# Halo copies of a four-layer convolution kernel: from three bursts per image to one or two copies per pair of tiles

## The chip, the cores and the metric

The kernel runs on one core of one Trainium2 chip. The metric is the device time of one launch in microseconds, as the median of several runs. The engines are named as in the profile: PE (TensorE), DVE (VectorE), ACT (ScalarE), POOL (GpSimd) and SP (SyncE, which only issues DMAs here).

## The reference

Four residual layers act on x of shape (T=4, B=8, N=512, D=512), float32; for the last three, the first axis counts images, the second channels, and 512 x 512 are rows and columns:

```
x = x + attention(group_norm(x))         # layer 0
x = x + conv13x13_depthwise(group_norm(x))   # layer 1, reflected borders
x = x + conv3x3_int8(group_norm(x))      # layer 2: x scaled by 127 / max|x| over all, rounded; weights likewise; plus bias
x = x + conv3x3(group_norm(x))           # layer 3: zero padding, plus bias
```

`group_norm` has 4 groups of 2 channels and takes mean and variance over a group's channels and all rows and columns of an image. So layer 3 of an image can begin only when layer 2 of that whole image is done.

## The kernel before

Layers 0 and 1 take the first 2590 us and are not touched. Layer 1 leaves its result in DRAM (`x2d`); layers 2 and 3 work on it together, in the function `layers23`.

An image of 512 rows is cut into 85 windows of 8 rows x 8 channels = 64 partitions; neighbouring windows start 6 rows apart. Two windows lie one above the other in the 128 partitions of a tile, two tiles make a pair, and an image has 22 pairs (`N_PAIRS`; the last holds one window). The result of layer 2 stays in SBUF in `x3`, a ring with places for 26 pairs (`RING`), since layer 3 follows 25 pairs behind (`N_PAIRS + LAG`).

The steps for one pair, with their lines:

- `load` (L949): two DMAs of 256 KB, issued by SP, bring the pair into one of six `x` buffers, five pairs ahead.
- `quantise`: POOL reorders the columns into `u` (L963, two copies, four `u` buffers), ACT scales them to `y` (L967), DVE rounds them to bf16 `xq` (L972).
- `layer2`: twelve matmuls (L988), then DVE adds the residual and writes `x3` (L993), and takes statistics (L996).
- `layer3`: POOL fills the two border columns (`edge`, L1059), TensorE does the fp32 matmuls (L1066), ACT adds the constant and writes `o` (L1075, six buffers), SP stores it (L1082, two DMAs of about 192 KB).

A 3 x 3 filter on a window of 8 rows gives 6 rows of results. So after layer 2 only the 6 inner rows of a window are right, and its first and last row (the halo) must come from the windows above and below before layer 3 reads them. The function `halos` does this inside SBUF, by DMAs that POOL issues (L1013 and L1014): the first row of each window is copied from the seventh of the window above, and the last row of the one above from the second of this window. One copy serves all windows of one class (the four places `c` in a pair) in a range of pairs; each moves 8 partitions x 2 KB per window. Where a range crosses the end of the ring, `split` cuts the copies into pieces.

Before, the halos of an image are issued in three ranges of pairs, 0 to 10, 11 to 18 and 19 to 21, each at once when its last pair is through layer 2:

```
chunks = [0, 11, 19, N_PAIRS]
if 0 <= t < T and p + 1 in chunks:
    halos(t, chunks[chunks.index(p + 1) - 1], p + 1)
```

After an image's last pair, `norm3` computes its norm in steps between the pairs: sums on DVE and TensorE, a power on POOL (L195), then DVE folds the norm into layer 3's weights (`band_t`, L1035), and TensorE and DVE make a constant (L1044, L1048).

The framework puts the instructions of each engine in an order of its own that keeps the dependences; each engine then runs its list strictly in that order. `n` counts the turns of the main loop: layer 2 of pair `n`, quantising of pair `n + 1`, layer 3 of pair `n - 25`.

Of the kernel before, what the change touches and what calls it, by code (L numbers as in the profile page):

```python
# [43 lines left out]
T, B, N, D, H = 4, 8, 512, 512, 8  # L44
# [20 lines left out]
W_IN, W_STEP, W_ALL = 8, 6, 85  # L65
N_PAIRS = (W_ALL + 3) // 4
# [6 lines left out]
def place(q):  # L73

    p, c = divmod(q, 4)
    return p, c // 2, (c % 2) ^ (c // 2)
# [816 lines left out]
def layers23(  # L893
    s, tc, x2d, out, ident, ind, mask2, avg_same, group_steps, m2, r2, most, w, early, pool
):
    nc = tc.nc
# [44 lines left out]
    def load(t, p):  # L941
        ahead[t, p] = xt = early["x"].tile([P, 2, D], F32, tag="x", name=f"x2_{t}_{p}")
        src = x2d[t]
        first, second = (dict(windows(k)) for k in (2 * p, 2 * p + 1))
        for a, q in first.items():

            n = 2 if a in second else 1
            step = second[a] - q if n == 2 else 1
            nc.sync.dma_start(  # L949
                xt[a * HALF : (a + 1) * HALF, :n, :],  # L950
                bass.AP(
                    src.tensor, src.offset + q * W_STEP * B * D,
                    [[D, HALF], [step * W_STEP * B * D, n], [1, D]],
                ),
            )

    def quantise(t, p):
        n, n_p = len(tiles(p)), HALF * len(windows(tiles(p)[-1]))
        x = ahead.pop((t, p))[:n_p, :n, :]
        u = early["u"].tile([P, 2, D], F32, tag="u", name="u2")  # L960
        y = early["y"].tile([P, 2, D], F32, tag="y", name="y2")
        for j in range(n):
            nc.gpsimd.tensor_copy(  # L963
                u[:n_p, j, :].rearrange("p (v g) -> p v g", g=PH),
                x[:, j, :].rearrange("p (g v) -> p v g", g=PH),
            )
        nc.scalar.activation(  # L967
            y[:n_p, :n, :], u[:n_p, :n, :], AF.Identity, bias=w["mr"][:n_p, t : t + 1],
            scale=w["r"][:n_p, t : t + 1],
        )  # L970
        xq = w["xq"][(t * N_PAIRS + p) % 3]
        nc.vector.tensor_scalar(  # L972
            xq[:n_p, :n, 2 : D + 2], y[:n_p, :n, :], ROUND, ROUND, op0=ALU.add, op1=ALU.subtract
        )
        ready[t, p] = u, xq

    def layer2(t, p):
        ks = tiles(p)
        n_p = HALF * len(windows(ks[-1]))
        u, xq = ready.pop((t, p))  # L980
        s0 = slot(t, p)
        st3 = w["st3"][t % 2]
        for j, k in enumerate(ks):
            ps = ps_2.tile([P, D], F32, tag="conv2", name="ps_conv2")
            for dx in range(3):
                for a, _ in windows(k):
                    half = slice(a * HALF, (a + 1) * HALF)
                    mm = nc.tensor.matmul(  # L988
                        ps[half, :], lhsT=w["band2"][half, 0, dx, :], rhs=xq[half, j, dx + 1 : dx + 1 + D],
                        start=dx == 0, stop=dx == 2,  # L990
                    )
            own = x3[:n_p, s0 + j, 1 : D + 1]
            nc.vector.scalar_tensor_tensor(  # L993
                own, ps[:n_p, :], w["inv"][:n_p], u[:n_p, j, :], op0=ALU.mult, op1=ALU.add
            )
            nc.vector.bn_stats(st3[:n_p, k, :], own)  # L996
        return mm.ins
# [3 lines left out]
    def halos(t, p0, p1):  # L1001


        for c in range(4):
            first = max(p0, 1) if c == 0 else p0
            n = min(p1, (W_ALL - c + 3) // 4) - first
            _, j, a = place(c)
            before, j_b, a_b = place(c + 3)
            for q0, q1, n_q in split(t, first, n, before - 1):
                here = pairs[a * HALF : (a + 1) * HALF, q0 : q0 + n_q, j, :]  # L1010
                there = pairs[a_b * HALF : (a_b + 1) * HALF, q1 : q1 + n_q, j_b, :]
                end = (W_IN - 1) * B
                nc.gpsimd.dma_start(here[:B], there[W_STEP * B : (W_STEP + 1) * B])  # L1013
                nc.gpsimd.dma_start(there[end : end + B], here[B : 2 * B])  # L1014

    def split(t, p, n, back):

        while n > 0:
            q0, q1 = slot(t, p) // 2, slot(t, p + back) // 2
            now = min(n, RING - q0, RING - q1)  # L1020
            yield q0, q1, now
            n, p = n - now, p + now

    def norm3(t):


        st3 = w["st3"][t % 2].rearrange("p k (h z) -> p (k h) z", z=3)
        nc.vector.tensor_scalar_add(st3[:, :, 1], st3[:, :, 1], w["b2"])
        m, r = yield from group_steps(
            st3.unsqueeze(1), 1, W2_N * 2, mask2, avg_same, ps_1, f"x3_{t}"  # L1030
        )
        zero = wpool.tile([P, 1], F32, tag="zero", name="zero")
        nc.vector.tensor_sub(zero, m, w["b2"])
        band = wpool.tile([P, 2, 3, HALF], F32, tag="band", name="band_t")
        nc.vector.scalar_tensor_tensor(  # L1035
            band, w["band3"], r, w["eye3"], op0=ALU.mult, op1=ALU.add
        )
        scaled = wpool.tile([P, 1], F32, tag="scaled", name="scaled")
        nc.vector.tensor_mul(scaled, zero, r)
        yield  # L1040
        ps = ps_1.tile([P, 1], F32, tag="misc", name="ps_const")
        for a in range(2):
            half = slice(a * HALF, (a + 1) * HALF)
            nc.tensor.matmul(  # L1044
                ps[half, :], lhsT=w["sum3"][half, a, :], rhs=scaled[half, :], start=True, stop=True
            )
        const = wpool.tile([P, 1], F32, tag="const", name="const")
        nc.vector.tensor_sub(const, w["b23"], ps)  # L1048
        norms[t] = zero, band, const
        yield  # L1050

    def layer3(t, p, zero, band, const):


        ks = tiles(p)
        s0 = slot(t, p)
        n_p = HALF * len(windows(ks[-1]))
        edge = x3[:n_p, s0 : s0 + len(ks), 0 : D + 2 : D + 1]
        nc.gpsimd.tensor_copy(edge, zero[:n_p].unsqueeze(2).to_broadcast([n_p, len(ks), 2]))  # L1059
        ps = [ps_3.tile([P, D], F32, tag="conv3", name="ps_conv3") for _ in ks]  # L1060
        for dx in range(3):
            for j, k in enumerate(ks):
                for a, q in windows(k):
                    half = slice(a * HALF, (a + 1) * HALF)
                    b = 1 if q == W_ALL - 1 else a ^ j
                    nc.tensor.matmul(  # L1066
                        ps[j][b * HALF : (b + 1) * HALF, :], lhsT=band[half, b, dx, :],
                        rhs=x3[half, s0 + j, dx : dx + D],
                        start=dx == 0, stop=dx == 2,
                    )  # L1070
        for j, k in enumerate(ks):
            q = 4 * p + 2 * j
            used = slice(HALF if q == W_ALL - 1 else 0, P)
            o = early["o"].tile([P, D], F32, tag="o", name="o3")
            nc.scalar.activation(o[used], ps[j][used], AF.Identity, bias=const[used])  # L1075
            row, n = q * W_STEP + 1, 2 * W_STEP
            at = 2 * B
            if q == 0:
                row, n, at = row - 1, n + 1, at - B
            if q == W_ALL - 1:  # L1080
                n, at = W_STEP + 1, HALF
            nc.sync.dma_start(  # L1082
                out[t, :, row : row + n, :].rearrange("c r w -> r c w"), o[at : at + n * B, :]
            )

    chunks = [0, 11, 19, N_PAIRS]
    n_all = T * N_PAIRS
    norms, norm = {}, iter(())  # L1090
    for n in range(n_all + N_PAIRS + LAG):
        if n < n_all:
            for m in range(6) if n == 0 else [n + 5]:
                if m < n_all:
                    load(*divmod(m, N_PAIRS))
            for m in range(2) if n == 0 else [n + 1]:
                if m < n_all:
                    quantise(*divmod(m, N_PAIRS))
            did = layer2(*divmod(n, N_PAIRS))
        next(norm, None)  # L1100
        t, p = divmod(n - 1, N_PAIRS)
        if 0 <= t < T and p + 1 in chunks:
            halos(t, chunks[chunks.index(p + 1) - 1], p + 1)
        if n >= N_PAIRS + LAG:
            t, p = divmod(n - N_PAIRS - LAG, N_PAIRS)
            with tc.issue_after(did):
                layer3(t, p, *norms[t])
        if n < n_all and n % N_PAIRS == N_PAIRS - 1:
            norm = norm3(n // N_PAIRS)
        next(norm, None)  # L1110
# [36 lines left out]
```

## Time and profile before

| What | Value |
|---|---|
| Time, median of 3 runs | 3078.7 us (3075.29 to 3078.77) |
| Span of the profiled execution | 3080.3 us |
| PE, DVE, POOL, ACT busy over the whole span | 95%, 73%, 34%, 16% |
| Layer 2 alone | about 2600 to 2698 us |
| Layers 2 and 3 together | about 2698 to 3003 us |
| Layer 3 alone | about 3003 to 3077 us |
| Halo copies | 126, of 16 to 176 KB, about 0.59 us of POOL each |

The busy shares are averages over stages with different limits: TensorE is full in layers 0 and 1 and less so afterwards. What the change can move is read in the last 480 us. "x<-x" in the DMA lists is a halo copy when POOL issues it, and a load of `x2d` (or of layer 1's input) when SP does.

### The profile page before, as it was taken

The numbers are of one execution on the slowest core, as the hardware profiler recorded it, in microseconds if no ns is written. First come the engines' busy times: TensorE is split into PE (matmuls) and PEld (weight loads), VectorE is DVE, ScalarE is ACT, GpSimd is POOL, SyncE is SP. The second block draws the span as 40 slices with busy tenths as digits, with TensorE's granted clock in tenths as the row PEclk, the third lists the DMA queues.
The fourth block names the chain that finished last, engine by engine and source line by source line (L and its number), as shares of the span: only waits on it lengthen the run. The fifth ranks groups of instructions, "written<-read, shape, count | busy, mean of one in ns | idle before, by whom it ended". The sixth has DMA issues, their size and how long they took to land. (4 is left out here: it accounts for less than half of the span.)

```text
span 3080.3 us, 38586 instructions
## 1 busy us (share of the span) xinstructions
PE 2917.2 (95%) x13993; PEld 1467.1 (48%) x13993; DVE 2246.8 (73%) x3761; ACT 481.6 (16%) x657; POOL 1056.4 (34%) x1995
## 2 busy tenths in 40 slices
PE   8999999999999999999999999998999997488789
PEld 6555555555555555555555555554333332144344
DVE  5997688688679768868967876886556556977660
ACT  1300010010000001001001000000112112254444
POOL 1242233333234223333323422332111114766661
PEclk9999999999999999999999999998999999899899
DMA  5221212212222221212211111115778776977775
GB/s 180 75 83 63 74 65 66 66 63 74 65 65 68 63 76 63 67 65 63 79 47 56 49 49 56 46 39 115 212 205 217 203 216 184 167 199 186 195 173 153
DMA packets 276212, 327.35 MB, mean 106 GB/s; under 512 B 24112, under 2 KB 171704, under 8 KB 275797
## 3 DMA queue, kind: packets, MB, share of 16 engines
q1 hardware_dynamic: 211930, 235.77, 28.1%
q0 software_dynamic: 24288, 62.35, 7.4%
q10 hardware_dynamic: 39803, 26.77, 2.9%
q8 instruction: 110, 1.80, 0.2%
q14 instruction: 81, 0.66, 0.1%
HBM read 210.60 MB, written 103.17 MB: 102 GB/s over the span
## 5 line engine op out<-in xcount | busy, mean ns | idle before, releaser
L464 PE MATMUL ps_in<-w_v,xn 128*128 128x512 f32 x1024 | 462.1, 600 | 2.4 <-issue 2.1
L464 PE MATMUL ps_in<-w_k,xn 128*128 128x512 f32 x1024 | 450.2, 592 | 1.1 <-DVE v_k L429 0.7
L464 PE MATMUL ps_in<-xn,w_q 128*128 128x512 f32 x1024 | 449.6, 592 | 0.2
L750 PE MATMUL ps_conv<-x,bt 112*64 112x512 f32 x2048 | 445.0, 593 | 0.0
L500 PE MATMUL ps_b<-toep,vtok 128*64 128x512 bf16 x3072 | 372.3, 383 | 0.0
L549 POOL COPY x1s<-x1s 128x2 f32<-128x2 f32 (+1 forms) x1024 | 227.2, 277 | 295.8 <-DVE x1s L538 295.8
L437 POOL TENSOR_TENSOR h_v<-h_v,c_v 128x512 f32<-128x512 f32 x96 | 123.1, 1283 | 578.9 <-DVE h_v L436 544.4
L412 ACT ACTIVATE h_q<-v_q,c_half 128x512 f32<-128x512 f32 x96 | 69.3, 722 | 1543.7 <-DVE v_q L408 1198.6
L527 PE MATMUL ps_out<-wp,so 128*128 128x512 f32 x1024 | 308.9, 444 | 0.0
L464 PEld LDWEIGHTS ps_in<-w_k,xn 128*128 128x128 f32 x1024 | 194.1, 190 | 222.4 <-issue 205.5
L464 PEld LDWEIGHTS ps_in<-xn,w_q 128*128 128x128 f32 x1024 | 191.8, 190 | 220.1 <-issue 213.1
L464 PEld LDWEIGHTS ps_in<-w_v,xn 128*128 128x128 f32 x1024 | 190.4, 191 | 216.8 <-issue 211.0
L750 PEld LDWEIGHTS ps_conv<-x,bt 112*64 112x64 f32 x2048 | 150.0, 135 | 286.4 <-issue 285.9
L1066 PE MATMUL ps_conv<-x,band_t 64*64 64x512 f32 x2040 | 269.6, 604 | 0.5 <-ACT o L1075 0.3
L500 PEld LDWEIGHTS <-vtok 128*64 128x64 bf16 x3072 | 209.4, 111 | 124.5 <-issue 4.5
L527 PEld LDWEIGHTS ps_out<-wp,so 128*128 128x128 f32 x1024 | 192.6, 188 | 94.1 <-issue 58.3
L963 POOL COPY u<-x 128x512 f32<-128x512 f32 (+1 forms) x172 | 198.5, 1189 | 104.0 <-issue 43.0
L988 PE MATMUL ps_conv<-xq,band 64*64 64x512 bf16 x1020 | 141.7, 411 | 87.7 <-DVE xq L972 86.6
L538 DVE SCALAR_TENSOR_TENSOR x1s<-v_p,xr 128x256 f32<-128x256 f32 x256 | 186.7, 769 | 15.1 <-DMA x<-x1s 3.9
L766 POOL DMA_DIRECT2D x<-xo x128 | 71.4, 565 | 340.6 <-ACT xo L757 326.2
L195 POOL TENSOR_TENSOR grstd_x<-grstd_x,neg_half 128x1 f32<-128x1 f32 (+1 forms) x28 | 21.7, 774 | 429.3 <-DVE grstd_x L194 429.3
L437 POOL TENSOR_TENSOR h_k<-h_k,c_k 128x512 f32<-128x512 f32 x96 | 124.5, 1297 | 117.5 <-DVE h_k L436 117.5
(174 smaller groups left out, 3551.1 us busy)
## 6 DMA issues: line engine op xcount, KB each, us to landing
x<-x SPq DMA_DIRECT2D x64, 917.0 KB
x<-x SPq DMA_DIRECT2D x168, 256.0 KB
x<-x1s POOLq DMA_DIRECT2D x128, 262.0 KB, 2.6
x<-in_x SPq DMA_DIRECT2D x128, 256.0 KB
xr<-in_x SPq DMA_DIRECT2D x128, 256.0 KB
out<-o SPq DMA_DIRECT2D x164, 192.0 KB
xs<-in_x SPq DMA_DIRECT2D x112, 256.0 KB
x<-xo ACTq DMA_DIRECT2D x128, 128.0 KB
```

The source lines that it names most:

```text
L412: nc.scalar.activation(h, v, AF.Identity, bias=c_col, scale=0.5)
L437: nc.gpsimd.tensor_add(h, h, c_twice[n])
L464: mm = nc.tensor.matmul(ps, lhsT=lhsT, rhs=rhs, start=k == 0, stop=k == NC - 1)
L500: nc.tensor.matmul(pb[two * DH : (two + 1) * DH, :], lhsT=v[:, c, h * DH : (h + 1) * DH], rhs=toep[z][:, h, u : u + N], start=c == 0 and z ...
L527: nc.tensor.matmul(ps, lhsT=so[:, k, c * P : (c + 1) * P], rhs=wpT[z][:, k, :], start=k == 0 and z == 0, stop=k == NC - 1 and z == 1,)
L538: nc.vector.scalar_tensor_tensor(own, v.rearrange("p (g v) -> p g v", g=PH)[:, two, :], 1.0, by_phase[:, two, :], op0=ALU.is_ge, op1=ALU.add,)
L549: nc.gpsimd.tensor_copy(x1[:, f, u : u + n], x1[:, fm, um - n + 1 : um + 1][:, ::-1])
L750: nc.tensor.matmul(ps[q * M1 : (q + 1) * M1, :], lhsT=bt[:, z, :], rhs=xt[:, w0 : w0 + N_PS1, z : z + NV], start=z == 0, stop=z == SHIFTS - 1,
L766: engine.dma_start(bass.AP(dst.tensor, dst.offset + (q * n_half * W1_OUT * B + b) * D + f * NV, [[B * D, W1_OUT], [W1_OUT * B * D, n_half] ...
L963: nc.gpsimd.tensor_copy(u[:n_p, j, :].rearrange("p (v g) -> p v g", g=PH), x[:, j, :].rearrange("p (g v) -> p v g", g=PH),)
L988: mm = nc.tensor.matmul(ps[half, :], lhsT=w["band2"][half, 0, dx, :], rhs=xq[half, j, dx + 1 : dx + 1 + D], start=dx == 0, stop=dx == 2,)
L1066: nc.tensor.matmul(ps[j][b * HALF : (b + 1) * HALF, :], lhsT=band[half, b, dx, :], rhs=x3[half, s0 + j, dx : dx + D], start=dx == 0, stop= ...
```

## The change

The halos of an image are issued for two halves, pairs 0 to 10 and 11 to 21. `halos` no longer issues its copies but yields them; the main loop keeps the list of a half and issues one or two of it per turn, so many that the list is empty after nine turns (the divisor is 11 - 2), before the next half begins. It is meant to keep POOL and the DMA engines from getting a whole range of copies at once.

```diff
-                nc.gpsimd.dma_start(here[:B], there[W_STEP * B : (W_STEP + 1) * B])
-                nc.gpsimd.dma_start(there[end : end + B], here[B : 2 * B])
+                yield here[:B], there[W_STEP * B : (W_STEP + 1) * B]
+                yield there[end : end + B], here[B : 2 * B]
...
-    chunks = [0, 11, 19, N_PAIRS]
+    n_chunk = N_PAIRS // 2
+    copies, at_once = [], 0
...
-        t, p = divmod(n - 1, N_PAIRS)
-        if 0 <= t < T and p + 1 in chunks:
-            halos(t, chunks[chunks.index(p + 1) - 1], p + 1)
+        if 0 < n <= n_all and n % n_chunk == 0:
+            t, p = divmod(n - n_chunk, N_PAIRS)
+            copies = list(halos(t, p, p + n_chunk))
+            at_once = -(-len(copies) // (n_chunk - 2))
+        for _ in range(min(at_once, len(copies))):
+            nc.gpsimd.dma_start(*copies.pop(0))
```

## The prediction

> **What bounds the kernel now.** I read the page for the order of the stages, then a table by stretches, because the change touches only the last 480 us. Layer 2 starts on TensorE at 2599.93 us. Up to 2698 layer 2 runs alone (25 pairs of tiles), up to 3003 layers 2 and 3 run together (63 pairs), then layer 3 alone (25 pairs). Columns: length, busy time of PE, PEld, DVE, ACT and POOL, TensorE clock, DMA share, GB/s.
>
> ```profile
> 2600.00:2698.00 98.00, 46.62 (x309) 19.37 (x312) 90.69 (x137) 31.78 (x27) 74.50 (x94) 0.82 0.81 151
> 2698.00:3003.00 305.00, 248.23 (x2158) 123.29 (x2156) 214.47 (x331) 143.36 (x179) 197.78 (x257) 0.90 0.79 190
> 3003.00:3077.00 74.00, 72.34 (x633) 36.31 (x629) 7.34 (x20) 36.50 (x54) 8.04 (x31) 1.00 0.58 158
> ```
>
> In undisturbed stretches of the TensorE timeline a pair takes 3.10 us in the first part (2608.44, 2611.54, 2614.65 and on) and 3.87 us in the second (2762.14, 2766.02, 2769.89). So 25 x 3.10 = 78 us became 98, and 63 x 3.87 = 244 us became 305: some 20 and 61 us are lost, while the tail is full. Whatever the change brings must come from these 81 us.
>
> Where are they? First ACT's timeline beside one burst of copies, and TensorE's next line (number in brackets: idle before, and who ended it):
>
> ```profile
> 2728.89 1.32 ACT L1075 ACTIVATE o<-ps_conv,const 128x512 f32<-128x512 f32 x2 [0.19 <-PE ps_conv L1066]
> 2733.75 0.69 ACT L1075 ACTIVATE o<-ps_conv,const 128x512 f32<-128x512 f32 x1 [3.54 <-DMA out<-o]
> 2735.34 0.69 ACT L1075 ACTIVATE o<-ps_conv,const 128x512 f32<-128x512 f32 x1 [0.90 <-DMA out<-o]
> 2743.87 0.69 ACT L1075 ACTIVATE o<-ps_conv,const 128x512 f32<-128x512 f32 x1 [7.84 <-DMA out<-o]
> ```
> ```profile
> 2748.83 2.34 PE L988 MATMUL ps_conv<-xq,band 64*64 64x512 bf16 x10 [8.44 <-DVE xq L972]
> ```
>
> The copies were issued at 2726.7 to 2732.5. After that the output DMAs land late; ACT (L1075) waits for one of the six `o` buffers; the activation `y` (L967) stands behind it on ACT, then `xq`, then TensorE. So the page's "DVE xq" releases a wait that DMA caused. The same picture ends the idle stretches before 2790.62 (7.0 us), 2860.02 (14.65), 2904.27 (4.9) and 2977.54 (15.2); each restart also runs some 2 us at a low clock. Second, the DMA queues in the first 34 us (no copies) and in the burst at 2634 to 2656, both with layer 2 alone (packets, MB, share of 16 engines):
>
> ```profile
> q1 hardware_dynamic: 2502, 4.57, 50.8%
> ```
> ```profile
> q0 software_dynamic: 864, 1.41, 64.5%
> q1 hardware_dynamic: 722, 1.31, 36.9%
> ```
>
> Loads: 4.57 MB in 0.508 x 34 = 17.3 us of all engines, 264 GB/s. Copies: 1.41 MB in 14.2 us, 99 GB/s: dear bytes. Third, GpSimd while the first image's norm is due:
>
> ```profile
> 2673.79 0.56 POOL L1013 DMA_DIRECT2D x<-x  x1 [0.83 <-DVE gsum_x L175]
> 2675.77 0.59 POOL L1014 DMA_DIRECT2D x<-x  x1 [1.42 <-DMA x<-x]
> 2678.27 0.55 POOL L1013 DMA_DIRECT2D x<-x  x1 [1.92 <-DMA x<-x]
> ...
> 2682.96 0.55 POOL L1014 DMA_DIRECT2D x<-x  x1
> 2683.52 2.05 POOL L963 COPY u<-x 128x512 f32<-128x512 f32 x2
> 2685.53 0.57 POOL L195 TENSOR_TENSOR grstd_x<-grstd_x,neg_half 128x1 f32<-128x1 f32 x1
> ```
>
> The variance (L194) is ready at 2676.75, but its power waits on GpSimd until 2685.53: eight copies, some waiting for earlier copies to land, stand before it. DVE then waits for the power at `band_t` (L1035), with the next `xq` behind that, and TensorE idles 11.1 us.
>
> **What the Trainium skill says.** "DMA: Bandwidth & Descriptors", section "Queues, rings and completion order": each DMA engine takes turns between the queues that have work, packet by packet. The trace agrees: q1 keeps moving in the burst, only slower. "SBUF — State Buffer", section "Door 1: The DMA port swizzle": bandwidth depends on how many of 16 ports the partitions reach; by its table a copy to 8 neighbouring partitions reaches two. The 99 against 264 GB/s fit this; no run here isolates it. Same page, "Who interferes with whom": DVE in its fast modes and GpSimd exclude each other. The trace shows `band_t` at 6.54 us beside GpSimd copies, against 0.6 us for the others ((8.4 - 6.5) / 3).
>
> **The change, part by part.**
>
> Number of issues. The ring has 26 places, an image 22 pairs. A half without a wrap needs 4 classes x 2 = 8 copies; a half with a wrap needs 3 + 2 + 2 + 2 = 9 pieces, 18 copies. Halves start at places 0, 11 | 22, 7 | 18, 3 | 14, 25; those at 22, 18 and 25 wrap. Sum 5 x 8 + 3 x 18 = 94 against 126 now (L1013 and L1014 x63 each). 32 fewer x 0.59 us (37.3 / 63) = 19 us of GpSimd, most of it beside TensorE work. Bytes stay the same.
>
> Order. The trace isn't in program order: 21 edge copies (L1059) run in one go at 2692 although the program has one per pair, and ten of the eighteen copies of image 1's first half stand at 2700 to 2716, eight pairs early. An instruction goes when it is ready and its engine is free; program order only breaks ties. Now eight copies with one place in the program precede the next `u` copies, hence the bursts. After the change the `u` copies come first and a copy takes the gaps; at 2700 to 2716 that gave one to three per pair. So I expect a spread, over some four to nine pairs, not an exact one per pair.
>
> First part, burst at n = 11. TensorE reaches pair 17 at 2655.53 instead of 2636.38 + 5 x 3.10 = 2651.9: 3.6 us lost. Spread, GpSimd has 2.6 us of `u` and 0.6 us of a copy per 3.1 us: about 0.1 x 8 = 1 us of loss. Gain some 2 us.
>
> First norm. Copies of pairs 11 to 18 are no longer issued just before it, so those at n = 22 wait for no landing (that was 1.42 + 1.92 + 0.95 + 1.00 us and more), and fewer stand before the power. If none does, the power comes at about 2677, 8 us sooner; if all eight do, at 2673 + 8 x 0.56 + 2.6 = 2680, 5 us sooner. I take 5, since those copies now collide with the start of layer 3.
>
> Second part: layer 3 of the images starts at 2698, 2807, 2920 and 3017.5, so three periods of 109, 113 and 97 us. The floor of TensorE is 21 x 3.87 + 2 = 83. DMA per full period: loads 22 x 0.524 = 11.5 MB and outputs 8.5 MB at 273 GB/s (q1 in the whole part: 50.12 MB in 60.2% of 305 us) make 73 us; copies 2.7 MB at 133 GB/s (q0: 7.38 MB in 18.2%) make 20 us. Together 93 us: when TensorE no longer stops, DMA is the bound, not TensorE. Today it is busy only 79%, because after each stop loads and outputs run dry (the DMA share is 0.13 at 2795 to 2800, and 0.23 at 2925 to 2930). Spread copies avoid most stops; at some 92% use a full period takes about 101 to 102 us. Gains: 8 and 11. The third period has few loads left (14 of 22 pairs: 7.3 MB), and the copies of image 3's second half, which now begin at 2962 just after another burst and belong to its 15 us stop, move mostly behind layer 2, where DMA is at 0.58: DMA need (7.3 + 8.5) / 0.273 + 2.2 / 0.133 = 74 us, so TensorE bounds it at some 80 us; with the norm and restarts 87. Gain 10.
>
> Added waits: a copy waits on GpSimd for the last pair's DVE work, with `u` copies queued behind it; this exists now (0.4 to 2.6 us). The last copy of a second half goes out at n = 29 or 30, its first reader is n = 35 or 36: five pairs, 19 us, against landings of at most 18.2 us now. Hidden, narrowly.
>
> Sum: 2 + 5 + 8 + 11 + 10 = 36 us; 3078.7 - 36 = 3043 us.
>
> **The rivals.** (a) TensorE becomes the only bound: 45 of the 61 us go and 14 of the 20: 3020 us. For it: copies at 2700 to 2716 caused no stop, and spread copies could move faster than 133 GB/s. Against it: the 93 us of DMA work. (b) The bursts form anew, since all copies of a half become ready at once: the second half now has 1.35 MB together instead of 1.0 and 0.35, and only the shorter norm remains: 3073 us, no measurable change. (c) Slower: copies between the `u` copies, 2.6 + 0.2 + 2 x 0.59 = 4.0 us of GpSimd per pair where a half wraps, against 3.87; more than eight in flight, which makes GpSimd wait for landings (it does in bursts now, up to 2.3 us a time) with `u` behind; and last copies landing after their readers are due. Five us in each of three periods gives 3094 us.
>
> **How the numbers follow.** Forecast 0.52, (a) 0.22, (b) 0.10, (c) 0.16. Faster by over 0.2% (6 us): the first two and a part of (b), 0.77; same 0.07; slower 0.16. The range runs from just under (a), 3016, to the milder half of (c), 3085.
>
> **What would show it.** Right: 94 halo copies in place of 126; ACT's wait at L1075 for the output DMA well under its 69.8 us; TensorE's wait at L988 for `xq` well under 86.6 us; the DMA share between 2698 and the end of layer 2 near 0.9; the first power before 2681; the tail still some 2.8 us per pair. Wrong: waits of layer 3's matmuls (L1066) for copies, GpSimd at its limit with ACT waiting for `u` (L963) more than now, or stops of 8 to 15 us in the old places.

## The result, and the profile after

| | before | after |
|---|---|---|
| Median (range) | 3078.67 us (3075.29 to 3078.77) | 3090.01 us (3085.03 to 3090.89) |
| Ratio of after to before, 95% interval | | 1.0036 [1.0019, 1.0054] |
| From layer 2's first matmul to the end, in the profile | 480.4 us | 487.9 us |

The change made the kernel slower by 0.36%, 11 us; 3043 us, 36 us less, had been forecast. The profile of after is of the fastest of its runs, and its layers 0 and 1 happened to end 4.6 us earlier (layer 2 starts at 2595.3 us, against 2599.9). So positions are compared from layer 2's start on. That time is cut into stages at layer 3's first matmul (L1066) of each image on TensorE; the last stage ends with TensorE's last matmul, 5.0 us before the end of the profile:

| Stage, us | before | after | difference | forecast difference |
|---|---|---|---|---|
| Layer 2 alone, up to layer 3 of image 0 | 98.1 | 108.8 | +10.7 | -7 |
| Layer 3 of image 0 to that of image 1 | 109.0 | 98.3 | -10.7 | -8 |
| Image 1 to image 2 | 113.1 | 101.8 | -11.3 | -11 |
| Image 2 to image 3 | 97.2 | 114.6 | +17.4 | -10 |
| Image 3 to the end of TensorE | 58.0 | 59.4 | +1.4 | 0 |

The differences of this one profile add up to 7.5 us; between the medians it is 11.3. The two middle stages did what was forecast. The first and the fourth lost 28 us together, where 17 us of gain were forecast, and these are the two stages to explain.

The table by stretches of after, with the columns of the one before (length; busy PE, PEld, DVE, ACT, POOL; clock, DMA share, GB/s):

```profile
2600.00:2698.00 98.00, 46.64 (x277) 17.64 (x275) 86.04 (x131) 27.59 (x23) 61.87 (x60) 0.74 0.72 133
2698.00:3003.00 305.00, 262.17 (x2170) 127.77 (x2172) 224.87 (x333) 144.92 (x182) 192.84 (x256) 0.92 0.86 197
3003.00:3077.00 74.00, 73.29 (x627) 35.75 (x624) 7.41 (x20) 32.42 (x51) 10.51 (x35) 0.97 0.59 148
```

In the first row the DMA share fell from 0.81 to 0.72, POOL's busy time from 74.5 to 61.9 us and the clock from 0.82 to 0.74: no engine is busier than before (TensorE has 46.6 us in both), and yet the stage takes longer. That points to a chain of steps that wait for each other, and not to a resource at its limit. In the second row the share rose, from 0.79 to 0.86, and the third is as full as it was. The same table for the middle, with the end of layer 2 left out, of before and then of after:

```profile
2700.00:2960.00 260.00, 218.43 (x1898) 109.35 (x1894) 189.53 (x294) 125.64 (x156) 175.40 (x229) 0.91 0.82 201
```
```profile
2700.00:2960.00 260.00, 233.24 (x1976) 116.10 (x1978) 204.29 (x302) 129.05 (x162) 181.50 (x242) 0.94 0.95 214
```

There the DMA engines went from 0.82 to 0.95 busy: the stops of TensorE behind the bursts are gone, but for one, which is shown below. The table of waits from 2595 us on (total, times, longest), of before and then of after:

```profile
PE ps_conv L988 <- DVE xq L972: 86.6, 26, 15.2
ACT o L1075 <- DMA out<-o: 69.8, 22, 13.6
ACT o L1075 <- PE ps_conv L1066: 34.7, 32, 2.0
```
```profile
PE ps_conv L988 <- DVE xq L972: 70.8, 31, 5.2
ACT o L1075 <- PE ps_conv L1066: 70.1, 25, 7.7
ACT o L1075 <- DMA out<-o: 53.4, 24, 9.6
```

TensorE's longest wait for `xq` fell from 15.2 to 5.2 us, but there are more waits. ACT waits less for the output DMA, and twice as long for layer 3's matmuls. So most of the long stops turned into many short ones.

**The short stops of image 0.** TensorE's timeline of after:

```profile
2628.69 1.50 PE L988 MATMUL ps_conv<-xq,band 64*64 64x512 bf16 x12 [1.61 <-DVE xq L972]
...
2643.92 2.77 PE L988 MATMUL ps_conv<-xq,band 64*64 64x512 bf16 x12 [3.95 <-DVE xq L972]
2649.43 2.77 PE L988 MATMUL ps_conv<-xq,band 64*64 64x512 bf16 x12 [2.75 <-DVE xq L972]
2654.95 2.10 PE L988 MATMUL ps_conv<-xq,band 64*64 64x512 bf16 x12 [2.75 <-DVE xq L972]
```

A pair takes 5.5 us (2643.92 to 2649.43 to 2654.95) in place of 3.1. Why is `xq` late? The DVE timeline of after, around the third of these pairs:

```profile
2651.03 0.75 DVE L993 SCALAR_TENSOR_TENSOR x<-ps_conv,inv,u 128x512 f32<-128x512 f32 x1 [1.66 <-PE ps_conv L988]
2651.82 0.69 DVE L996 BATCH_NORM_STATS2 st<-x 128x6 f32<-128x512 f32 x1
2652.43 0.73 DVE L993 SCALAR_TENSOR_TENSOR x<-ps_conv,inv,u 128x512 f32<-128x512 f32 x1
2653.20 0.69 DVE L996 BATCH_NORM_STATS2 st<-x 128x6 f32<-128x512 f32 x1
2653.81 1.08 DVE L972 TENSOR_SCALAR xq<-y 128x1024 bf16<-128x1024 f32 x1
```

and its input in the ACT timeline:

```profile
2643.96 1.24 ACT L967 ACTIVATE y<-u,mr_own,r_own 128x1024 f32<-128x1024 f32 x1 [4.61 <-DVE xq L972]
2649.47 1.24 ACT L967 ACTIVATE y<-u,mr_own,r_own 128x1024 f32<-128x1024 f32 x1 [4.27 <-DVE xq L972]
```

There are two `y` buffers, and each `y` here waits for the rounding that frees one; so the `y` of 2643.96 is read two roundings later, at 2653.81. It was done at 2645.20, 8.6 us before, and DVE stood idle for 1.66 us ahead of 2651.03. The rounding did not lack its operand: it stands in DVE's list behind four instructions, the first of which waits for TensorE. TensorE in turn waits for the rounding. So TensorE and DVE take turns: rounding, matmuls, additions and statistics, next rounding. Before, the list had the rounding of the next pair first. The DVE timeline of before:

```profile
2632.56 0.67 DVE L972 TENSOR_SCALAR xq<-y 128x1024 bf16<-128x1024 f32 x1
2633.15 1.40 DVE L993 SCALAR_TENSOR_TENSOR x<-ps_conv,inv,u 128x512 f32<-128x512 f32 x2
2634.47 1.27 DVE L996 BATCH_NORM_STATS2 st<-x 128x6 f32<-128x512 f32 x2
2635.66 0.67 DVE L972 TENSOR_SCALAR xq<-y 128x1024 bf16<-128x1024 f32 x1
```

**The short stops at the end of layer 2.** ACT's timeline of after:

```profile
2988.12 1.26 ACT L1075 ACTIVATE o<-ps_conv,const 128x512 f32<-128x512 f32 x2 [6.64 <-issue]
2989.28 1.24 ACT L967 ACTIVATE y<-u,mr_own,r_own 128x1024 f32<-128x1024 f32 x1
2998.22 1.26 ACT L1075 ACTIVATE o<-ps_conv,const 128x512 f32<-128x512 f32 x2 [7.71 <-PE ps_conv L1066]
```

and TensorE's in the same place:

```profile
2991.29 2.34 PE L988 MATMUL ps_conv<-xq,band 64*64 64x512 bf16 x10 [3.27 <-DVE xq L972]
2993.86 4.31 PE L1066 MATMUL ps_conv<-x,band_t 64*64 64x512 f32 x22
3001.39 2.34 PE L988 MATMUL ps_conv<-xq,band 64*64 64x512 bf16 x10 [3.23 <-DVE xq L972]
```

Here the same thing happens on ACT: the outputs (L1075) stand ahead of the next pair's `y`, and they wait for layer 3's matmuls, which on TensorE stand behind layer 2's. The chain is output, `y`, `xq`, layer 2, layer 3, output: 10.1 us a pair (2991.29 to 3001.39) in place of 3.87. POOL issued its last `u` at 2977.16 us, so no input was missing.

**One stop of the old kind.** Just before, pair 81 of layer 2 follows pair 80 only after 15.1 us (2947.21 to 2962.35). ACT waits there for an output DMA, with the DMA engines 0.94 busy (2942 to 2960 us), and layer 3's matmuls start again only when that output is done:

```profile
2953.04 0.69 ACT L1075 ACTIVATE o<-ps_conv,const 128x512 f32<-128x512 f32 x1 [9.56 <-DMA out<-o]
```
```profile
2953.83 2.06 PE L1066 MATMUL ps_conv<-x,band_t 64*64 64x512 f32 x4 [5.13 <-issue]
```

This stop is also there in e2 below, where the order is mended (14.8 us between the same pairs, 2930.39 to 2945.14), and it is gone in e8, which has no copies (3.9 us). So mending the order does not remove it.

**The lists themselves.** The order of each engine's list is fixed when the kernel is compiled. Two counts show what moved: for every pair of layer 2, how many later roundings stand on DVE ahead of its addition (L993), and for every turn of layer 3, how many later `y` stand on ACT ahead of its output (L1075). Call this count the lookahead. The instructions of both traces run in exactly this order. One digit per pair, 22 to an image; the ACT rows begin with turn 25, and the last digit of a row is always 0, since no pair follows:

```
DVE, roundings of later pairs ahead of L993 of pair n, n = 0, 1, ...
before   1111111111111021111110 1011222222221022223210 1001222222210222223210 1001222222221022223210
after    1111111111111000000021 1001111132222222222122 2101111132222222221122 2101111132221100000010

ACT, y of later pairs ahead of L1075 of turn n, n = 25, 26, ...
before   3444444321044443210112 4444333210444443210112 4444444321044443210
after    2222443433343332443210 2222444344333322443210 2222444322111000010
```

A zero means that the lookahead is gone for that pair. Before has single or double ones. After has a run of seven on DVE at pairs 13 to 19, where TensorE takes 5.5 us a pair on the mean, and six at pairs 80 to 85, with four on ACT at turns 82 to 85; the pairs behind these four, 83 to 86, take 6.8, 8.9, 9.0 and 10.1 us. The diff touches neither engine: only POOL's copies changed, and the order of the others moved with them.

### The profile page after: what moved, and what is told of

Same layout as the page of the kernel before. It is cut to its first block, busy times and chain, and to the rows that moved or that the text cites. A ratio compares the mean times of both kernels' runs of the same rounds, so it can differ in the third digit from the quotient of the medians.

```text
span 3083.2 us, 38484 instructions
## 1 busy us (share of the span) xinstructions
PE 2934.6 (95%) x13993; PEld 1470.5 (48%) x13993; DVE 2256.5 (73%) x3761; ACT 478.0 (16%) x657; POOL 1041.3 (34%) x1963
## 5 line engine op out<-in xcount | busy, mean ns | idle before, releaser
L1066 PE MATMUL ps_conv<-x,band_t 64*64 64x512 f32 x2040 | 274.5, 613 | 12.4 <-ACT o L1075 6.8
L963 POOL COPY u<-x 128x512 f32<-128x512 f32 (+1 forms) x172 | 201.7, 1203 | 114.3 <-issue 62.7
L988 PE MATMUL ps_conv<-xq,band 64*64 64x512 bf16 x1020 | 154.2, 432 | 76.2 <-DVE xq L972 70.8
L538 DVE SCALAR_TENSOR_TENSOR x1s<-v_p,xr 128x256 f32<-128x256 f32 x256 | 186.4, 768 | 14.8 <-DMA x<-x1s 3.5
L1066 PEld LDWEIGHTS ps_conv<-x,band_t 64*64 64x64 f32 x2040 | 118.5, 137 | 116.7 <-issue 92.9
```

Of the source, the lines that this page charges most:

```text
L538: nc.vector.scalar_tensor_tensor(own, v.rearrange("p (g v) -> p g v", g=PH)[:, two, :], 1.0, by_phase[:, two, :], op0=ALU.is_ge, op1=ALU.add,)
L963: nc.gpsimd.tensor_copy(u[:n_p, j, :].rearrange("p (v g) -> p v g", g=PH), x[:, j, :].rearrange("p (g v) -> p v g", g=PH),)
L988: mm = nc.tensor.matmul(ps[half, :], lhsT=w["band2"][half, 0, dx, :], rhs=xq[half, j, dx + 1 : dx + 1 + D], start=dx == 0, stop=dx == 2,)
L1066: nc.tensor.matmul(ps[j][b * HALF : (b + 1) * HALF, :], lhsT=band[half, b, dx, :], rhs=x3[half, s0 + j, dx : dx + D], start=dx == 0, stop= ...
```

## The experiments

Two theories. In theory A the two losses come from the order of DVE's and ACT's lists, and the copies, once spread, do what the prediction said. In the rival, theory B, the order is only a side effect: the copies between POOL's `u` instructions and in the DMA queues hold up `u`, `y` or `xq`, so that spread copies cost more than bursts. If A holds, putting the rounding back in front, with every copy left where it is, must mend the losses. If B holds, it mends nothing.

Each kernel is compared with the kernel before on the same chip (3077.0 to 3077.9 us), and the ratios are against that. The experiments ran on three chips, so a difference of a few us between two of them is not clear. The table of stages stands after the last of them.

### The rounding ahead of the addition (e1_xq_first)

An edge of order alone, on top of after: DVE's addition of pair n is issued after the rounding of pair n + 1. No instruction is added.

```diff
-        nc.vector.tensor_scalar(
+        rounded = nc.vector.tensor_scalar(
...
-            nc.vector.scalar_tensor_tensor(
-                own, ps[:n_p, :], w["inv"][:n_p], u[:n_p, j, :], op0=ALU.mult, op1=ALU.add
-            )
+            with tc.issue_after(before):
+                nc.vector.scalar_tensor_tensor(
+                    own, ps[:n_p, :], w["inv"][:n_p], u[:n_p, j, :], op0=ALU.mult, op1=ALU.add
+                )
...
-            did = layer2(*divmod(n, N_PAIRS))
+            did = layer2(*divmod(n, N_PAIRS), rounded)
```

> The changed kernel, with one ordering edge more per pair: on DVE, the instruction that writes pair n into the ring (L993) comes after the rounding of pair n+1 (L972). Copies, their places on GpSimd and all work stay. In the order of the changed kernel the rounding of the next pair stands behind the statistics of the pair before for pairs 13 to 19 of image 0 and for 80 to 85. Theory A (the order is the loss): pairs 13 to 19 go back from 5.4 to about 3.2 us, 7 x 2.2 = 15 us; pairs 80 to 85 stay slow, since ACT's order has the same fault there. About 3075 us. Rival B (the copies delay loads and u copies on GpSimd and the DMA engines, whatever the order): no change, 3090 us.

Measured: 3074.62 us, ratio 0.9984 [0.9977, 0.9992]. Layer 2 alone takes 92.8 us (after: 108.8). TensorE's timeline in the place where it took 5.5 us a pair (lines below L972 move down by one or two):

```profile
2647.20 1.50 PE L989 MATMUL ps_conv<-xq,band 64*64 64x512 bf16 x12 [1.64 <-DVE xq L972]
2650.32 1.50 PE L989 MATMUL ps_conv<-xq,band 64*64 64x512 bf16 x12 [1.62 <-DVE xq L972]
```

The pair is back at 3.12 us and the twelve matmuls at 1.50 us, while POOL's trace has the same copies and `u` in the same order as after's up to there. So the loss in image 0 is the order of DVE. The end of layer 2, where ACT's zeros are left, is still slow: 110.4 us between images 2 and 3 (after: 114.6), with pairs 9.0 us apart in the same timeline:

```profile
2978.36 1.28 PE L989 MATMUL ps_conv<-xq,band 64*64 64x512 bf16 x10 [3.26 <-DVE xq L972]
...
2987.34 2.34 PE L989 MATMUL ps_conv<-xq,band 64*64 64x512 bf16 x10 [3.22 <-DVE xq L972]
```

### And the scaling ahead of the outputs (e2_xq_y_first)

As e1, and layer 3 of a turn, its outputs on ACT with it, is issued after the `y` of the next pair:

```diff
-        nc.scalar.activation(
+        scaled = nc.scalar.activation(
...
-            with tc.issue_after(did):
+            with tc.issue_after(did), tc.issue_after(scaled):
```

> As the run before, and also on ACT: the outputs of a turn (L1075) come after the scaling of pair n+1 (L967). Theory A: the six pairs at 8 to 10 us near the end of layer 2 go to about 4.5 us, a further 20 to 25 us: about 3050 us, and the gain of the spread copies in images 1 and 2 stays (periods of 98 and 102 us between the starts of layer 3). Rival B: 3085 to 3090 us.

Measured: 3052.8 us, ratio 0.9913 [0.9898, 0.9928]. The period between images 2 and 3 falls from 110.4 to 91.8 us, and the one before it from 104.5 to 99.2. TensorE's timeline at the end of layer 2:

```profile
2952.91 1.25 PE L989 MATMUL ps_conv<-xq,band 64*64 64x512 bf16 x10
...
2956.79 1.25 PE L989 MATMUL ps_conv<-xq,band 64*64 64x512 bf16 x10
```

3.88 us a pair, with no wait. Two edges of order, no instruction more or less, turn the change from 0.36% slower into 0.87% faster. Theory B could not give this: POOL's order of copies and `u` is the same in the traces of e1 and e2, and DVE's order of roundings and additions too. What differs is ACT's list, where the zeros are gone.

### Spread only in the middle (e3_spread_middle)

Another way to take the runs of zeros away, without an edge: the first half of image 0 and both halves of image 3 go out at once, as bursts, and only those between are spread.

```diff
-            at_once = -(-len(copies) // (n_chunk - 2))
+            at_once = -(-len(copies) // (n_chunk - 2)) if n_chunk < n < 7 * n_chunk else len(copies)
```

> The changed kernel without ordering edges, but the first half of image 0 and everything from pair 77 on are issued at once; the five halves between are spread as in the change. Its order has no run of pairs with the rounding behind the statistics. Theory A: image 0 as long as before or a little shorter, the gain in images 1 and 2 kept, the last period near that of the kernel before: 3055 to 3062 us. Rival B (spread copies cost in themselves): no better than 3080 us.

Measured: 3063.05 us, ratio 0.9948 [0.9933, 0.9962]. In its compiled lists no two zeros follow each other on either engine. Layer 2 alone takes 91.5 us and the period between images 2 and 3 100.2. It came out 1 us above the forecast. That agrees with A: where the run of zeros is gone, the loss of image 0 is gone, and most of that of the last period (after: 114.6). In its place one stop of 17.4 us, before 2955.30, stands behind the burst of image 3. The run says nothing of B by itself, since the copies moved as well.

### Two halves, but as bursts (e4_halves_at_once)

The ranges of the change without its spreading:

```diff
-            at_once = -(-len(copies) // (n_chunk - 2))
+            at_once = len(copies)
```

> Two halves per image as in the change, but each issued at once when its last pair is through: 94 copies, no spread. Theory A, with its second part that bursts are what stops TensorE in images 1 and 2: the order is that of bursts, so no slow run of pairs, but the stops of 8 to 15 us stay: 3065 to 3080 us, and slower than the run with the middle spread. Rival C (the fewer copies are the gain, not the spread): as fast as the run with the middle spread or faster.

Measured: 3073.1 us, ratio 0.9982 [0.9975, 0.9989]. Layer 2 alone takes 89.5 us (before: 98.1): two ranges for three bring that without any spreading. With them the first norm's power comes 82.3 us after layer 2's start, against 85.6 in before and 96.9 in after. The first two image periods stay at 112.7 and 111.0 us, and the long stops are there as in before. TensorE's timeline of e4:

```profile
2741.87 2.34 PE L988 MATMUL ps_conv<-xq,band 64*64 64x512 bf16 x10 [8.81 <-DVE xq L972]
...
2850.41 2.34 PE L988 MATMUL ps_conv<-xq,band 64*64 64x512 bf16 x10 [12.70 <-DVE xq L972]
```

So the two parts of the change do different things: the ranges mend image 0, and the spreading mends the periods from image 0 to 2 (98.3 and 101.8 in after, 102.1 and 102.9 in e3).

### The edges without the change (e5_before_ordered)

The kernel before with both edges of e2.

> The kernel before with both ordering edges (next pair's rounding ahead of L993, next pair's scaling ahead of L1075) and its three bursts. Theory A: the order of the bursts had few such faults, so the gain is small, and the long waits of ACT for output DMAs after each burst stay: 3060 to 3072 us. Rival D (the edges alone are the gain of the second run, the spread adds nothing): 3053 us or less.

Measured: 3084.27 us, ratio 1.0023 [1.0017, 1.003]: a little slower, where a gain was expected. TensorE still stops (7.9, 9.6, 8.2, 10.0 and 12.1 us at 2744, 2786, 2856, 2902 and 2980 us) and ACT waits 69.7 us for the output DMA, as in before (69.8). So the stops behind the bursts are there without any run of zeros, and the edges bring nothing against them. Why the kernel loses 7 us was not settled. The edges paid only with the spread copies.

### Three ranges, spread (e6_thirds_spread)

The ranges of before, with the copies spread over some nine turns. Its compiled DVE list has the longest runs of zeros of all: pairs 13 to 25, 44 to 47, 66 to 69 and 80 to 87.

```diff
-    n_chunk = N_PAIRS // 2
+    chunks = [0, 11, 19, N_PAIRS]
...
-        if 0 < n <= n_all and n % n_chunk == 0:
-            t, p = divmod(n - n_chunk, N_PAIRS)
-            copies = list(halos(t, p, p + n_chunk))
-            at_once = -(-len(copies) // (n_chunk - 2))
+        t, p = divmod(n - 1, N_PAIRS)
+        if 0 <= t < T and p + 1 in chunks:
+            copies += halos(t, chunks[chunks.index(p + 1) - 1], p + 1)
+            at_once = -(-len(copies) // 9)
```

> No ordering edges; the three ranges of the kernel before, its 126 copies spread one or two per pair. In its order the rounding of the next pair stands behind the statistics for 13 pairs of image 0 (13 to 25) and for eight at the end (80 to 87), and for four in a row at the start of images 2 and 3. Theory A, counting 2.3 us for each of the 13 and the same last period as in the changed kernel: some 13 us more than it in image 0, 4 to 8 us more in images 1 and 2 together: about 3105 us. Rival B (cost per copy on GpSimd): 32 more issues x 0.59 us, at most 10 of it seen: 3090 to 3100 us.

Measured: 3113.7 us, ratio 1.0115 [1.01, 1.013], the slowest of all. Layer 2 alone takes 120.8 us, and TensorE's timeline has the 5.5 us step from 2644 to 2661 and again later (2697.47 to 2702.99):

```profile
2655.39 2.77 PE L988 MATMUL ps_conv<-xq,band 64*64 64x512 bf16 x12 [2.75 <-DVE xq L972]
2660.91 2.77 PE L988 MATMUL ps_conv<-xq,band 64*64 64x512 bf16 x12 [2.75 <-DVE xq L972]
```

More zeros, more loss, at the pairs where the list has them. That holds in the first two image periods too, which are 14 and 10 us longer than after's: behind the zeros at 44 to 47, the additions (L993) of pairs 45 to 48 follow each other after 6.7, 8.7, 9.1 and 9.1 us. The forecast had 4 to 8 us for these two periods together, and came out 9 us too low.

### e3 with both edges (e7_middle_ordered)

> The middle spread (first half of image 0 and everything from pair 77 on at once) with both ordering edges. Theory A: order is mended already, so the rest of the gain is the spread of the last halves: near the second run, 3050 to 3058 us.

Measured: 3057.83 us, ratio 0.9937 [0.9925, 0.9949]. The edges bring e3 little (the intervals of e3 and e7 overlap), against 37 us to after (3090.01 to 3052.8): they are worth what the zeros cost. With the order held in both, spreading every half (e2) looks 5 us better than spreading the middle ones alone, but these intervals touch as well.

### No copies (e8_no_copies_ordered)

e2 with an empty list of copies (`copies = []`).

> Leaves out all halo copies, with both ordering edges: layer 3 reads the first and last row of each window as layer 2 left them. Shows what the copies still cost in the best order. Without them the DMA need of an image is 73 us, under TensorE's 83, so every period should be near 85 to 88 us and the part with layer 2 alone 80 to 86: theory A gives 3005 to 3020 us. If the copies cost nothing any more: 3050 us.

Measured: 2999.34 us, ratio 0.9747 [0.9735, 0.976], 6 us under the lower end of the forecast. The copies still cost 53 us in the best version. That includes what the lists gain without them: the lookahead of e8 is 2 at most pairs on DVE and 4 at nearly all turns on ACT, more than e2 has at most places. The middle stretch of e2 and then of e8 shows what bounds:

```profile
2700.00:2960.00 260.00, 233.63 (x2002) 116.67 (x2000) 207.96 (x304) 134.63 (x168) 175.99 (x235) 0.95 0.93 217
```
```profile
2700.00:2960.00 260.00, 254.97 (x2342) 128.69 (x2338) 195.26 (x326) 150.29 (x196) 146.41 (x176) 1.00 0.70 203
```

Without the copies TensorE is 98% busy and the DMA share is 0.70; with them TensorE is 90% busy and the share is 0.93. (The last 25 us of e8's stretch have no layer 2 any more; up to 2930 us the shares are 0.73 and 0.95.) So the prediction's bound for the image periods, DMA and not TensorE, holds, and without the copies a full period takes 87 to 88 us (forecast for TensorE's floor: 83).

### The copies from other queues (e9_ordered_sp, e10_ordered_act)

e2 with `nc.sync.dma_start`, then with `nc.scalar.dma_start`, in place of `nc.gpsimd.dma_start`. It frees POOL, but the copy and its wait then stand in the queue that issues loads and outputs, or in ACT's list.

> The second run (spread as in the change, both ordering edges), with the halo copies issued by SP instead of GpSimd. If what the copies still cost (3053 against 2999 us without them) is the transfers on the DMA engines: little change, 3045 to 3060 us. If it is GpSimd's 0.6 us per copy and its waits for landings: 3015 to 3035 us. If copies waiting for DVE hold up the loads and stores behind them on SP: over 3060 us.

> The same with ACT as the issuer. ACT is some 45% busy in this part, but every copy that waits for DVE holds up the scaling and the outputs. Transfers as the cost: 3045 to 3065 us; GpSimd's part as the cost: 3020 to 3040 us.

Measured: 3088.58 us, ratio 1.0033 [1.0021, 1.0045] from SP, and 3084.01 us, 1.0017 [1.0009, 1.0025] from ACT; 36 and 31 us behind e2. The first is the third case of its forecast; the second lies above both of its cases. The waits of the first, then of the second:

```profile
POOL u L963 <- DMA x<-x: 118.6, 39, 7.2
```
```profile
ACT o L1077 <- DMA x<-x: 78.2, 20, 7.5
```

In the first, `u` waits for loads (in that kernel "x<-x" in SP's queue is both load and halo copy). In the second, outputs wait behind copies. Meanwhile the DMA engines run emptier: their share between 2700 and 2960 us is 0.78 and 0.79, against 0.93 in e2. Of the three issuers POOL did best. But the lists changed here too: the lookahead is 1 at all pairs on DVE in e9 and at nearly all in e10, and mostly 1 or 2 on ACT, where e2 has up to 3 and 4. So the issuer's part and the order's are not separated.

### The stages of all kernels

In us, as in the first table; the last column but one is the time from layer 2's first matmul to the end of the profile, about 5 us more than the five stages; the last is the median's ratio to before.

| Kernel | layer 2 alone | 0 to 1 | 1 to 2 | 2 to 3 | 3 to end | whole | ratio |
|---|---|---|---|---|---|---|---|
| before | 98.1 | 109.0 | 113.1 | 97.2 | 58.0 | 480.4 | 1 |
| after | 108.8 | 98.3 | 101.8 | 114.6 | 59.4 | 487.9 | 1.0036 |
| e1: rounding first | 92.8 | 101.1 | 104.5 | 110.4 | 63.2 | 477.1 | 0.9984 |
| e2: rounding and scaling first | 92.8 | 100.6 | 99.2 | 91.8 | 63.1 | 452.4 | 0.9913 |
| e3: spread in the middle | 91.5 | 102.1 | 102.9 | 100.2 | 61.0 | 462.7 | 0.9948 |
| e4: halves at once | 89.5 | 112.7 | 111.0 | 96.1 | 61.3 | 475.6 | 0.9982 |
| e5: before, both edges | 98.2 | 111.9 | 116.2 | 98.5 | 58.0 | 487.9 | 1.0023 |
| e6: thirds, spread | 120.8 | 112.2 | 111.8 | 110.0 | 57.3 | 517.1 | 1.0115 |
| e7: e3, both edges | 93.8 | 100.6 | 102.1 | 97.8 | 60.8 | 460.0 | 0.9937 |
| e8: no copies, both edges | 84.0 | 88.4 | 86.9 | 79.2 | 58.0 | 401.5 | 0.9747 |
| e9: e2, copies from SP | 89.5 | 103.0 | 111.7 | 109.7 | 72.3 | 490.7 | 1.0033 |
| e10: e2, copies from ACT | 93.1 | 117.3 | 112.4 | 96.8 | 62.7 | 486.9 | 1.0017 |

e2 is the best that still computes everything: 25 us under before.

## Why the prediction was wrong

The step that failed is "Order". It took POOL's list as the only one that the change rewrites, and DVE's and ACT's as given, so the order of these two has no term in the sum. It cost 37 us (3090.01 against 3052.8 with both edges). It even said that "program order only breaks ties", and drew from this only where copies would stand between the `u` instructions. That part came true: the copies stand one to three per pair. What it missed is that the same rearrangement put DVE's rounding behind the additions for pairs 13 to 19 and 80 to 85, and ACT's `y` behind the outputs at the end. No resource and no transfer shows this in advance, and the lists of before had no more than two zeros in a row to warn of it.

By the steps of the sum:

- **Number of issues.** 94 copies in place of 126, as counted; they take 57.2 us of POOL in place of 74.5, 17 us less (forecast: 19).
- **First part, burst at n = 11: gain 2.** This term has the wrong sign. It looked at POOL and DMA only. At the seven zeros a pair takes 5.5 us, and the whole stage lost 10.7 us where this term and the next one had 7 of gain. With the rounding in front (e1) the stage gains 5.3.
- **First norm: power before 2681, gain 5.** It came at 2692.22, or 96.9 us after layer 2's start against 85.6: the pairs ahead of it were late, not the copies in its way. In e4, where the order is as before, it comes at 82.3. So fewer copies before the norm do help, by about 3 us of the 5.
- **Image periods, gains 8 and 11.** Right in mechanism and size: 10.7 and 11.3, at a DMA share of 0.95 (forecast 0.92). The periods forecast at 101 to 102 us took 98.3 and 101.8. e4 and e5, whose bursts keep the long stops with and without the edges, show that it is the spreading that does it.
- **Third period, gain 10.** The period took 114.6 us, where 87 were forecast. Most of this is the same failure on ACT and DVE at the end of layer 2: with both edges (e2) it takes 91.8, a gain of 5.4. The stop of 14.8 us between pairs 80 and 81, which is there in e2 too, is more than what is missing to 87; the forecast took the 15 us stop of this place as gone.
- **Tail, no change.** +1.4 in after, but +5.1 in e2. There the eight large copies of the last half (144 KB) are issued between 2969.75 and 2981 us, and the tail begins at 2979.4; ACT then waits four times for output DMAs (2.40, 2.83, 2.12 and 2.68 us, up to 2991.6). The prediction moved these copies there at no cost. Why after pays less for them was not settled.

With the order mended, then, the sum of the prediction's own terms is -28 us in e2's trace (-5.3, -8.4, -13.9, -5.4 and +5.1) where it said -36, and -25 us between the medians. Rival (a), TensorE as the only bound, is refuted by the DMA share of 0.95 and by e8. Rival (b), new bursts, did not happen while layers 2 and 3 ran together: up to the last pairs no more than three copies stand in a row on POOL. Rival (c), at 3094 us, came near the measured 3090 by luck, for its mechanism was not there: it put the loss into each image period, from POOL or late copies, and two of the three periods got faster. ACT's wait for `u`, its sign of POOL at the limit, fell from 111.0 to 71.6 us, and no wait of layer 3's matmuls that the trace of after can name is for a copy.

The order is shown as the cause by e1 and e2, which add no work and take no copy away, and by e6, which makes it worse. What is not shown is why the framework chose these orders.

## What to carry to other kernels

When a change moves instructions on one engine and the framework chooses the order, compare the compiled lists of all engines before pricing anything: count for each consumer how many of the next producers stand ahead of it, and look for runs of zeros. In these traces, lost lookahead shows as an instruction that starts long after its operand was ready (8.6 us here), behind others that wait on the engine it feeds, while DVE, ACT, POOL and the DMA engines are less busy than before. Where the lookahead matters, hold it with an edge of order, so that a change elsewhere cannot take it away.

## What the runs showed of the hardware

- The same twelve bf16 matmuls took 1.50 us where 1.6 us of idle lie between pairs and 2.10 to 2.77 us where 2.75 us do (granted clock 1.00 at 2608 to 2624 us and 0.61 at 2645 to 2661 in after). So this serial chain paid twice: for the handovers, and for slower matmuls in it.
- Spreading the copies did not make their bytes cheaper. From the DMA queues between 2700 and 2960 us (packets, MB, share of 16 engines), first before and then after:

```profile
q0 software_dynamic: 4319, 6.16, 17.1%
```
```profile
q0 software_dynamic: 4874, 7.48, 22.1%
```

That is 6.16 MB in 0.171 x 260 us, 139 GB/s, and 130 GB/s when spread. What the traces show of the gain is that the DMA engines stand idle less (a share of 0.95 in place of 0.82).
- A rounding of 0.67 us took 2.99 us at 2631.05 in after, with POOL's `u` copies and issues running beside it (2.04 us of `u` from 2631.44, an issue from 2633.42). What made it so long was not isolated.
